# A list scheduler's price for entering the row strips: one figure for all, or one for the maxima and one for the exponentials

## The chip, the core and the metric

The kernel runs on one NeuronCore of a Trainium2 chip. The metric is the device time of one execution in microseconds (us). Three executions of the kernel before gave 1381.47, 1381.62 and 1383.63 us, median 1381.62.

## What is computed

The reference is one transformer layer on `x` of 2 x 2048 x 256 in float32: layer norm, causal attention with 16 heads of 16 (projections with biases, rotary positions), a residual sum, layer norm again, and a gated feed-forward of width 704 whose operands are rounded in blocks of 16 to a four-bit grid (E2M1), with another residual sum.

```python
x = x + attention(layernorm(x), Wq, bq, Wk, bk, Wv, bv, Wo, bo)
n = layernorm(x)
h = silu(fp4_linear(n, w_gate)) * fp4_linear(n, w_up)
x = x + fp4_linear(h, w_down)
# attention: softmax(mask(rope(q) @ rope(k).T / 4)) @ v, head by head
# fp4_linear(x, w) = fp4(x) @ fp4(w).T
```

## The kernel before, in words

The two sequences are cut into chunks of 512 rows, four for each, and the 16 heads into four groups of four. A slot is one group of one chunk; there are 32 of them. In each slot the scores are computed twice.

The first time they serve for the row maxima only (`max_steps`, called **the maxima** here). One task of this kind is two matmuls (line 1094, tile `sc`), one on the upper and one on the lower 64 rows of the TensorE array, each into a PSUM bank of its own. Two DVE reductions (line 1118) read the banks. At the diagonal four small masking matmuls (line 1062) belong to the task. When all maxima of a slot are found, DVE splits them into two bfloat16 parts, PE turns them (line 1175, tile `ptm`) and ACT copies them to `mT`.

The second time they are computed transposed, for the softmax (`value_steps`, called **the exponentials**). One task is two bfloat16 matmuls that subtract the maxima (line 1227) and two float32 score matmuls on top of them (line 1235), all on 64 rows, tile `sx`; ACT takes the exponential of both banks (line 1250). Four more matmuls (line 1283, tile `av`, **the values**) then multiply with `v` on all 128 rows and 32 columns each.

Everything else on PE (projections, turnings, the feed-forward's `pg` and `pd`) uses the whole array. A matmul thus runs in one of three tilings, named in the code `"strip"` (64 rows x 128 columns: maxima and exponentials), `"value"` and `"whole"`. All PSUM results but `av` rotate through seven banks; a task of maxima or exponentials takes two of them, other tasks one.

Nothing of this is issued as the loops run. Each step is given to `Plan.add` with its engine, a reckoned cost, what it reads and writes, its due time, and for PE the tiling. `Plan.ordered` is a list scheduler: it keeps a clock for each engine and a list of the tasks that are ready, and picks the next one. For the picked engine it takes the tasks that could begin within `PATIENCE` of the earliest, and of these the one with the smallest rank, the due time; on PE, `CHANGE` is added to a task whose tiling is not that of the task before. When a PE task does change the tiling, `ENTER[t.tiling]` is added to the reckoned start. The instructions of each engine are then issued in the order found and are tied to it. The engines run at their own pace; only the order is kept. Due times come from the place of the slot, so maxima of the next slot, exponentials of this one, projections and feed-forward are woven into each other.

In the first 170 us of the reckoned time, `kept_busy` (line 488) puts matmuls without use into PE time that the plan finds idle, one for each 0.2 us.

The figures that the change touches, as they stand before it:

```python
CHANGE = 0.1
PATIENCE = 0.03
ENTER = dict(strip=0.11, value=0.08, whole=0.08)
```

Of the kernel before, what the change touches and what calls it, by code (L numbers as in the profile page):

```python
# [65 lines left out]


AHEAD = 3
CHANGE = 0.1
FEED_M = 0.0  # L70
FEED_V = 0.0
PATIENCE = 0.03
TURN = 0.3
ISSUE = 0.46

# [29 lines left out]
PE, DVE, ACT, POOL, SP = "PE", "DVE", "ACT", "POOL", "SP"  # L105
# [6 lines left out]
    SP: {PE: 0.05, DVE: 0.05, ACT: 0.05, POOL: 0.05, SP: 0.05},  # L112
}

ENTER = dict(strip=0.11, value=0.08, whole=0.08)


class Thing:
# [13 lines left out]


class Task:
    __slots__ = "engine cost run due tiling late left ready end after new kinds start idle".split()


class Plan:
# [7 lines left out]

    def add(
        self, engine, cost, run, reads=(), writes=(), due=0.0, books=(), tiling="whole", feeds=0.0,
        late=0.0,
    ):  # L150
        t = Task()
        t.engine, t.cost, t.run, t.due = engine, cost, run, due - feeds

        t.tiling, t.late = tiling, late or 1.0 * (engine == SP)
        t.left, t.ready, t.end, t.after, t.new = 0, 0.0, None, [], []
        before = set()
        for thing in reads:
            assert thing.writers, (engine, due)
            before.update(thing.writers)
        for thing in writes:  # L160
            before.update(thing.writers)
            before.update(thing.readers)
        for thing in reads:
            thing.readers.append(t)
            thing.whole().users.append(t)
        for thing in writes:
            thing.writers, thing.readers = [t], []
            thing.whole().users.append(t)

        for thing in (*writes, *books):  # L170
            whole = thing.whole()
            if whole.kind and not whole.there:
                whole.there = True
                whole.users.append(t)
                whole.number = self.made[whole.kind] = self.made.get(whole.kind, -1) + 1
                t.new.append(whole)
        t.kinds = {}
        for thing in t.new:
            t.kinds.setdefault(thing.kind, []).append(thing)
        before.discard(t)  # L180
        for b in before:
            b.after.append(t)
        t.left = len(before)
        self.tasks.append(t)
        return t

    def ordered(self):

        waiting = {e: [] for e in HOP}
        for n, t in enumerate(self.tasks):  # L190
            if not t.left:
                waiting[t.engine].append((t.due, n, t))
        number = {t: n for n, t in enumerate(self.tasks)}
        free = dict.fromkeys(HOP, 0.0)
        rooms = {kind: [] for kind in ROOM}
        turn = dict.fromkeys(ROOM, 0)
        tiling = "whole"
        dues = sorted(((t.due, n) for n, t in enumerate(self.tasks)), reverse=True)
        done = set()
        out = []  # L200

        def vacancy(kind, n, to):

            held = rooms[kind]
            n -= ROOM[kind] - len(held)
            if n <= 0:
                return 0.0, []
            some = []
            for thing in held:
                if all(u.end is not None for u in thing.users):  # L210
                    at = max(
                        u.end + (u.late if u.engine != SP else 0.0) + HOP[u.engine][to]
                        for u in thing.users
                    )
                    some.append((at, thing.number, thing))
            if len(some) < n:
                return None
            some = sorted(some)[:n]
            return some[-1][0], [thing for *_, thing in some]

        while len(out) < len(self.tasks):
            while dues and dues[-1][1] in done:
                dues.pop()
            horizon = dues[-1][0] + (AHEAD if dues[-1][0] < self.near_end else 50.0)
            choice = None
            for e, queue in waiting.items():
                queue.sort(key=lambda x: x[:2])
                able = []
                vacant = {}
                for due, n, t in queue:  # L230
                    if due > horizon or len(able) > 30:
                        break
                    at = max(t.ready, free[e])
                    for kind, some in t.kinds.items():
                        if kind not in ANY_TURN and some[0].number != turn[kind]:
                            break
                        key = kind, len(some)
                        if key not in vacant:
                            vacant[key] = vacancy(*key, e)
                        if vacant[key] is None:  # L240
                            break
                        at = max(at, vacant[key][0])
                    else:
                        able.append((at, due, n, t))
                if not able:
                    continue
                first = min(at for at, *_ in able)
                if choice and first > choice[0] + 1e-9:
                    continue

                def rank(x):
                    at, due, n, t = x
                    return due + (CHANGE if e == PE and t.tiling != tiling else 0.0)

                pick = min((x for x in able if x[0] <= first + PATIENCE), key=rank)
                if choice is None or pick[0] < choice[0]:
                    choice = pick
            at, due, n, t = choice
            e = t.engine
            waiting[e].remove((due, n, t))  # L260
            for kind, some in t.kinds.items():
                for thing in vacancy(kind, len(some), e)[1]:
                    rooms[kind].remove(thing)
                rooms[kind] += some
                turn[kind] += len(some)
            if e == PE:
                if t.tiling != tiling:
                    at += ENTER[t.tiling]
                tiling = t.tiling
                t.start, t.idle = at, at - free[e]  # L270
            if e == SP:
                free[e] = at + ISSUE * t.late
                t.end = free[e] + t.cost
            else:
                t.end = free[e] = at + t.cost
            done.add(n)
            out.append(t)
            for a in t.after:
                a.left -= 1
                late = t.late if a.engine != e and e != SP else 0.0  # L280
                a.ready = max(a.ready, t.end + late + HOP[e][a.engine])
                if not a.left:
                    waiting[a.engine].append((a.due, number[a], a))
        self.span = max(t.end for t in out)
        return out
# [29 lines left out]
def layer_kernel(  # L315
# [88 lines left out]
    def lay_pick(due):  # L404
        def run():
            for strip in range(2):
                rows = slice(strip * STRIP, (strip + 1) * STRIP)
                nc.vector.tensor_copy(pick[rows], ident[rows, rows])

        add(DVE, 0.5, run, [fixed], [pick_], due)  # L410
# [660 lines left out]
    maxima, max_ = {}, {}  # L1071
# [3 lines left out]
    def max_steps(b, c, g):  # L1075
# [7 lines left out]
        def one(i, kc, d, due):  # L1083
# [22 lines left out]
            def reduced(h):  # L1106
# [21 lines left out]
                "strip",  # L1128
                FEED_M,
                0.07,  # L1130
            )
            for h in range(2):
                own = Thing(of=parts if c else mx)
# [60 lines left out]
        for i in range(TPC):  # L1194
            for kc in range(c + 1):
                for d in range(2):
                    steps.append(lambda due, i=i, kc=kc, d=d: one(i, kc, d, due))
# [529 lines left out]
    for n in range(slots + 1):  # L1727
        cost = 0.4 * (order[n // NG][1] + 1) if n < slots else 0
# [28 lines left out]
    for m in range(1, NBLK * len(order)):  # L1757
        k, blk = divmod(m, NBLK)
        at, use = place[2 * m - 2], place[2 * m]
# [21 lines left out]
    ready = [divided[NG * k + NG - 1] + 0.01 for k in range(len(order))]  # L1781
    ready[0] = max(ready[0], WEIGHTS + 0.2)
    end = place[slots + 1]
    at = 0
    for k in range(len(order) - 1):
# [3 lines left out]
        at = lo + (until - lo) / (last_k - k)  # L1789
        if NG * k + 10 < slots:  # L1790
            at = min(at, lo + (place[NG * k + 10] - lo) / 0.85)
        if k == len(order) - 2:
            at = end + LATE
# [6 lines left out]
    at = [0, 0, 1.5, 5.5, 8, 11, 12, 14.5, 17.3, 20, 26.7, 27.2, 28.2]  # L1800
# [167 lines left out]
```

## Time and profile before

| | |
|---|---|
| runs, us | 1381.47, 1381.62, 1383.63 (median 1381.62) |
| span of the profiled execution, us | 1378.9 |
| its own device time | not given apart from the runs; the median stands 2.7 us above the span |
| mean granted TensorE clock | 0.979 |
| PE busy | 1317.6 us, 96% |
| DVE busy | 1115.1 us, 81% |
| ACT busy | 749.9 us, 54% |
| GpSimd busy | 538.4 us, 39% |

PE is TensorE's matmuls, PEld its weight loads, which overlap the matmuls. Busy time of PE includes matmuls that overlap one another, so it does not show whether PE works at its best rate. The distances between the starts of successive matmuls show that better. In a timeline row, x2 or x4 says how many matmuls of one kind were merged, and the first number is the start of the first one.

### The profile page before, as it was taken

Reading aid. Unit: us, or ns where it says so; the run is one execution under the profiler, and the core shown is the slowest. Engines: PE = TensorE matmul, PEld = TensorE weight load, DVE = VectorE, ACT = ScalarE, POOL = GpSimd, SP = SyncE. Lnnn points to the kernel's source line nnn. Section 1 sums busy time; section 2 is a strip of 40 time slices with the busy share of each in tenths; the row PEclk is TensorE's granted clock in tenths of the full one; section 3 lists DMA queues with packets and bytes.
Section 4 is the critical chain, followed back from the end, with each engine's and each line's share of the span. In section 5 each row is a group of like instructions: output and inputs, shape, how many; then the busy total and the mean of one; then the engine's idle time right before and its main releaser. Section 6 shows DMA issues by size and latency. Waiting matters only on the chain.

```text
span 1378.9 us, 27730 instructions
## 1 busy us (share of the span) xinstructions
PE 1317.6 (96%) x10408; PEld 656.7 (48%) x10408; DVE 1115.1 (81%) x2415; ACT 749.9 (54%) x1670; POOL 538.4 (39%) x685
## 2 busy tenths in 40 slices
PE   7988999999999999999998999999999999999977
PEld 4544444444544444444454555444454444444445
DVE  7788989988889998875479888996878988894296
ACT  2542655556555566557643455554655566667711
POOL 4754634434423334314345644432442332320360
PEclk8998999999999999999999999999999999999988
DMA  2653432411221401221343414240130130000000
GB/s 88 133 134 100 103 94 58 104 33 55 62 41 44 107 20 41 64 45 51 89 113 94 108 44 97 66 95 22 47 86 17 43 81 13 9 9 9 9 1 19
DMA packets 61887, 84.39 MB, mean 61 GB/s; under 512 B 14772, under 2 KB 30520, under 8 KB 61752
## 3 DMA queue, kind: packets, MB, share of 16 engines
q1 hardware_dynamic: 61744, 82.61, 24.2%
q8 instruction: 82, 1.34, 0.4%
q14 instruction: 53, 0.43, 0.1%
q10 hardware_dynamic: 8, 0.00, 0.0%
HBM read 55.09 MB, written 27.49 MB: 60 GB/s over the span
## 4 chain that ended last, share of the span: by engine, by line
PE 65%; DVE 19%; POOL 5%; issue 5%; DMA 3%; ACT 2%; SPq 0%; POOLq 0%; DVEq 0%; ACTq 0%
PE av L1283 15%; PE sc L1094 9%; PE pg L1575 9%; PE sx L1227 8%; DVE parts L1118 7%; PE sx L1235 7%; PE pd L1669 6%; PE pj L837 3%; PE pth L1434 2%; PE po L1519 1%; PE pv L1019 1%; DVE scale L582 1%; DVE step L609 1%; DVE mx L1118 1%; PE sc L1062 1%
## 5 line engine op out<-in xcount | busy, mean ns | idle before, releaser
L1250 ACT ACTIVATE ex<-sx 128x512 f32<-128x512 f32 (+3 forms) x1280 | 592.8, 538 | 345.9 <-PE sx L1235 202.1
L1118 DVE TENSOR_REDUCE parts<-sc 128x1 f32<-128x512 f32 (+3 forms) x1152 | 637.9, 611 | 65.2 <-PE sc L1094 46.6
L1235 PE MATMUL sx<-qT,kT 64*128 64x512 f32 (+3 forms) x1280 | 335.6, 521 | 0.0
L1283 PE MATMUL av<-ex,v 128*32 128x512 f32 (+3 forms) x2560 | 301.3, 543 | 0.0
L1094 PE MATMUL sc<-kT,qT 64*128 64x512 f32 (+3 forms) x1280 | 280.3, 425 | 8.9 <-DMA kT<-parts 2.5
L1227 PE MATMUL sx<-mT,less 64*128 64x512 bf16 (+3 forms) x1280 | 246.5, 355 | 5.4 <-DVE parts L1118 1.6
L1094 PEld LDWEIGHTS sc<-kT,qT 64*128 64x128 f32 x1280 | 132.8, 188 | 168.1 <-DVE parts L1118 51.2
L1227 PEld LDWEIGHTS <-less 64*128 64x128 bf16 x1280 | 66.5, 94 | 213.3 <-issue 205.5
L590 POOL TENSOR_SCALAR inv<-inv 128x16 f32<-128x16 f32 (+2 forms) x82 | 17.7, 216 | 373.0 <-DVE inv L586 341.2
L1235 PEld LDWEIGHTS sx<-qT,kT 64*128 64x128 f32 x1280 | 131.3, 196 | 9.0 <-issue 6.8
L1669 PE MATMUL pd<-wdT,hrT 128*128 128x256 f32 (+1 forms) x384 | 103.9, 411 | 1.5 <-ACT hrT L1438 1.0
L1283 PEld LDWEIGHTS av<-ex,v 128*32 128x32 f32 x2560 | 52.6, 108 | 70.8 <-issue 60.4
L1669 PEld LDWEIGHTS pd<-wdT,hrT 128*128 128x128 f32 (+1 forms) x384 | 70.4, 197 | 29.1 <-issue 16.0
L889 POOL TENSOR_TENSOR t<-t,cs 128x512 f32<-128x512 f32 x31 | 39.9, 1286 | 110.2 <-DVE t L883 104.8
L1575 PE MATMUL pg<-wgT,xT 128*128 128x352 f32 x224 | 76.9, 476 | 0.9 <-ACT xT L1438 0.8
L837 PE MATMUL pj<-xnT,wqkT 128*128 128x512 f32 x128 | 73.8, 672 | 3.5 <-DVE v L1028 1.7
L1118 DVE TENSOR_REDUCE mx<-sc 128x1 f32<-128x128 f32 (+3 forms) x128 | 54.3, 477 | 25.8 <-PE sc L1062 25.8
L1575 PE MATMUL pg<-wuT,xT 128*128 128x352 f32 x224 | 74.4, 471 | 0.1
L1062 PE MATMUL sc<-pick,mask_q 64*128 64x64 bf16 x1024 | 67.3, 198 | 0.0
L615 POOL TENSOR_TENSOR h<-h,step 128x704 f32<-128x704 f32 x28 | 47.2, 1686 | 48.8 <-DVE step L612 41.0
L1601 ACT ACTIVATE h<-pg 128x352 f32<-128x352 f32 x64 | 29.9, 467 | 64.6 <-PE pg L1575 56.5
L547 POOL TENSOR_SCALAR ve<-mv 128x1 f32<-128x1 f32 x64 | 12.6, 197 | 130.4 <-DVE mv L543 127.1
(163 smaller groups left out, 1614.8 us busy)
## 6 DMA issues: line engine op xcount, KB each, us to landing
qT<-parts SPq DMA_DIRECT2D x120, 128.0 KB
kT<-parts SPq DMA_DIRECT2D x120, 128.0 KB
parts<-high SPq DMA_DIRECT2D x30, 256.0 KB
parts<-t SPq DMA_DIRECT2D x30, 256.0 KB
sums<-avs SPq DMA_DIRECT2D x28, 256.0 KB
cs<-in_rope_dram SPq DMA_DIRECT2D x8, 512.0 KB
xin<-in_L_attn_x_dram SPq DMA_DIRECT2D x28, 128.0 KB
y<-sums SPq DMA_DIRECT2D x28, 128.0 KB
```

The source lines that it names most:

```text
L615: queue.tensor_tensor(src(), src(), st["step"], ALU.add)
L837: nc.tensor.matmul(got["pj"], lhsT=wqkT[:, k, i, cols], rhs=xnTs[b, c][:, k, :], start=(k == 0), stop=(k == KE - 1),)
L889: (nc.gpsimd if early and i == 0 else queue).tensor_tensor(swapped, swapped, angles[b, c][:, 1, :], ALU.mult)
L1062: nc.tensor.matmul(sc[h][:, col + at : col + at + STRIP], lhsT=strips(mask, h, half), rhs=strips(pick, h), start=False, stop=(half == 1),)
L1094: nc.tensor.matmul(sc[h][:, :cols], lhsT=strips(qT, h, d, slice(i * P, (i + 1) * P)), rhs=strips(kT, h, duo, slice(0, cols)), start=True, ...
L1118: nc.vector.tensor_reduce(dst, got[0][h][:, :cols], AX.X, ALU.max)
L1227: nc.tensor.matmul(sc[h][:, off:], lhsT=strips(less[d], h), rhs=strips(mT, h, slice(off, CH)), start=True, stop=False,)
L1235: nc.tensor.matmul(sc[h][:, off:], lhsT=strips(kT, h, duo, slice(jj, jj + P)), rhs=strips(qT, h, d, slice(off, CH)), start=False, stop=(j ...
L1250: nc.scalar.activation(st[j, d][:, h, off:], got[0][h][:, off:], AF.Exp, scale=HD**-0.5)
L1283: nc.tensor.matmul(st["av"][SLOT * s : SLOT * (s + 1), off:], lhsT=v[:, at : at + SLOT], rhs=st[j, d][:, h, off:], start=(j == 0), stop=(j ...
L1575: nc.tensor.matmul(got[half], lhsT=split("xrT")[:, k, :], rhs=wT[:, k, half * IH : (half + 1) * IH], start=(k == 0), stop=(k == KE - 1),)
L1669: nc.tensor.matmul(st["pd"], lhsT=st["hrT"][:n, k, :], rhs=wdT[:n, k, :], start=(k == 0), stop=(k == KI - 1),)
```

## The change

The price of entering a tiling becomes a field of the task. A task of maxima now carries the figure `maxima`, 0.19; exponentials and the few other strip tasks carry `strip`, now 0.09 instead of 0.11. The ranking adds this price of the task itself where it added 0.1 to any change of tiling. `PATIENCE`, which holds for all engines, becomes 0.06. No instruction that computes is added or taken away; the order may change on all engines, and with it the useless matmuls of `kept_busy`.

```diff
-CHANGE = 0.1
 FEED_M = 0.0
 FEED_V = 0.0
-PATIENCE = 0.03
+PATIENCE = 0.06
...
-ENTER = dict(strip=0.11, value=0.08, whole=0.08)
+ENTER = dict(strip=0.09, maxima=0.19, value=0.08, whole=0.08)
...
     def add(
         self, engine, cost, run, reads=(), writes=(), due=0.0, books=(), tiling="whole", feeds=0.0,
-        late=0.0,
+        late=0.0, enter=None,
     ):
         t = Task()
+        t.enter = ENTER[enter or tiling]
...
-                    return due + (CHANGE if e == PE and t.tiling != tiling else 0.0)
+                    return due + (t.enter if e == PE and t.tiling != tiling else 0.0)
...
                 if t.tiling != tiling:
-                    at += ENTER[t.tiling]
+                    at += t.enter
...
                 "strip",
                 FEED_M,
                 0.07,
+                "maxima",
             )
```

More of the change, by code (lines that the diff above doesn't have):

```diff
@@ L134 @@
 class Task:
-    __slots__ = "engine cost run due tiling late left ready end after new kinds start idle".split()
+    __slots__ = "engine cost run due tiling late left ready end after new kinds start idle enter".split()
 class Plan:
```

## Prediction

> **What bounds the kernel.** I read the page first: the busy shares, then the chain of work that ended last, then the costliest groups.
>
> ```profile
> PE 1317.6 (96%) x10408; PEld 656.7 (48%) x10408; DVE 1115.1 (81%) x2415; ACT 749.9 (54%) x1670; POOL 538.4 (39%) x685
> ...
> PE 65%; DVE 19%; POOL 5%; issue 5%; DMA 3%; ACT 2%; SPq 0%; POOLq 0%; DVEq 0%; ACTq 0%
> ...
> L1250 ACT ACTIVATE ex<-sx 128x512 f32<-128x512 f32 (+3 forms) x1280 | 592.8, 538 | 345.9 <-PE sx L1235 202.1
> L1118 DVE TENSOR_REDUCE parts<-sc 128x1 f32<-128x512 f32 (+3 forms) x1152 | 637.9, 611 | 65.2 <-PE sc L1094 46.6
> ```
>
> PE carries most of the chain, DVE a fifth. One reduction takes 611 ns, one exponential 538, each twice per task. The busy time by stretches of 69 us shows where DVE is as full as PE:
>
> ```profile
> 207.00:276.00 69.00, 67.23 (x534) 33.48 (x532) 66.02 (x146) 35.38 (x80) 32.12 (x39) 1.00 0.36 81
> ...
> 414.00:483.00 69.00, 66.70 (x500) 31.88 (x496) 65.33 (x131) 38.41 (x81) 26.67 (x34) 1.00 0.31 76
> ...
> 1242.00:1311.00 69.00, 68.54 (x577) 30.77 (x574) 23.57 (x49) 51.19 (x116) 12.20 (x16) 1.00 0.03 9
> ```
>
> Columns are length, PE, PEld, DVE, ACT and POOL busy, clock, DMA share and rate. DVE leaves 3.0 and 3.7 us of 69 free in the first two, 45 in the last. So a gain on PE counts nearly everywhere, but in some stretches DVE stands close behind.
>
> The timeline of PE then shows what entering the strips costs:
>
> ```profile
> 488.12 0.39 PE L1094 MATMUL sc<-kT,qT 64*128 64x512 f32 x2
> 488.35 0.39 PE L1227 MATMUL sx<-mT,less 64*128 64x512 bf16 x2
> ...
> 488.91 1.13 PE L1519 MATMUL po<-woT,y 128*128 128x256 f32 x4
> 489.97 0.50 PE L1094 MATMUL sc<-kT,qT 64*128 64x512 f32 x2
> 490.32 0.39 PE L1227 MATMUL sx<-mT,less 64*128 64x512 bf16 x2
> 490.35 0.58 PE L1235 MATMUL sx<-qT,kT 64*128 64x512 f32 x2
> 490.77 0.40 PE L1094 MATMUL sc<-kT,qT 64*128 64x512 f32 x2
> 491.10 1.07 PE L1283 MATMUL av<-ex,v 128*32 128x512 f32 x8
> 492.10 0.39 PE L1227 MATMUL sx<-mT,less 64*128 64x512 bf16 x2
> 492.13 0.58 PE L1235 MATMUL sx<-qT,kT 64*128 64x512 f32 x2
> 492.55 0.40 PE L1094 MATMUL sc<-kT,qT 64*128 64x512 f32 x2
> ```
>
> From the first matmul of a task to that of the next, maxima inside strips take 0.23 (488.12 to 488.35); maxima behind a whole-array product take 0.35 (489.97 to 490.32). Exponentials take 0.45 in both cases (490.32 to 490.77 in strips, 492.10 to 492.55 behind the values). Medians over all such undivided tasks of 512 columns in the trace, taken the same way: maxima followed by exponentials 0.237 in strips (48 behind exponentials), 0.340 behind values (34) or whole (43); exponentials followed by maxima 0.458 in strips (43 behind maxima), 0.458 behind values (60) and whole (39). The change of tiling itself shows in the distance before: a last value matmul stands 0.433 from a next value task, 0.525 from exponentials, 0.522 from maxima. Leaving is alike: exponentials followed by values take 0.549 for 0.458. So each change costs 0.091, and maxima that enter cost 0.103 on top.
>
> **What the new order does.** The two programs' orders of PE, counted (useless matmuls as whole): strips are entered 528 times before, 256 by maxima and 272 by exponentials; after, 516 times, 120 and 396. Values are entered 310 and 318 times, whole 304 and 296. All changes: 1142 and 1130. The matmuls are the same, but for 140 useless ones instead of 139, so I take the clock as kept. Where work lies on the large scale hardly moves: after each further 128 value matmuls the counts of maxima differ by at most 8 of 1280, of feed-forward products by 3 or fewer, and what follows the last value is the same count.
>
> **Removed.** 136 fewer entries by maxima x 0.103 = 14.0 us. 12 fewer changes x 0.091 = 1.1 us. Sum -15.1 us, all on PE. The 124 entries that exponentials take over cost nothing beyond the change, counted already: they begin with two bfloat16 loads of 94 ns mean, while the maxima begin with float32 loads of 188 (rows of the weight loads). The Trainium skill's "TensorEngine Tiling (Array Packing)", section Key Properties, says that changing the tiling mode drains TensorE, and makes no difference by what enters. By that rule alone only the 12 changes would count, and the sum so far would be -1.1 us.
>
> **Added: waits for banks.** Exponentials first means maxima later and in clumps. Runs of a single task of maxima fall from 423 to 263, runs of two rise from 68 to 142, of three from 23 to 24, longer ones from 2 to 4. I took each task's excess over the quickest quarter of its like (same shape, same neighbours) in the trace: 113 us in all, of which 45 at seams among maxima, exponentials and values. Around a run of one the excess is 0.105 us, of two 0.226, of three 0.658. Priced so, the runs come to 76 us before and 78 after: +2. The other end: I counted, in both orders, how often one of the seven banks is wanted again after less unstalled PE work than its readers need (611 or 538 ns each, plus 0.35 for the hand-over by the kernel's own table). That is 246 times before and 302 after, 23% more, mostly at the exponentials. 23% of 45 us is +10. The waits of the weight loads say that such waits exist:
>
> ```profile
> PEld sc L1094 <- DVE parts L1118: 51.2, 83, 1.5
> PEld sc L1094 <- ACT ex L1250: 35.6, 65, 1.1
> ```
>
> They are time without a load, much of it hidden behind running matmuls, so not a price. I take +6, midway, since runs ignore what stands between them and the count ignores that one wait relieves the next. "TensorEngine Tiling (Array Packing)", section Gotcha 1: PSUM Pressure, speaks against the change in the same direction: row tiling puts more pressure on the banks. It gives no price.
>
> **Added: the end of a slot.** Behind the last maxima stand the split and the turning (line 1175), for which the first exponentials wait. PE has under 3 us of other work in between in 5 of 32 slots before, in 7 after. PE stood 5.3 us idle at line 1175 in all, about 1.06 for each short slot: 0 to +2, taken +1, as other slots gain room.
>
> **PATIENCE.** It lets the list reckon up to 0.03 us more idle time before a pick, on DVE, ACT, GpSimd and SP too. The engines themselves only follow the order, and no row prices that. Below: 0, where queued values and products cover it. Above: about 174 changed picks (124 entries and 50 more maxima inside strips) x 0.03 = +5. Taken 0, the nearer end, since a wait drawn only in the plan is none on the chip. Below nothing it could avoid a further change, but those are counted already. SP's queue swaps a few neighbours among `parts`, `xin` and weight loads, far ahead of their use; 0, unless a `qT` or `kT` comes late, as one 2.5 us wait of PE for `kT` did before.
>
> **Sum.** -15.1 + 6 + 1 + 0 = -8.1; ends -15.1 + 2 + 0 + 0 = -13.1 and -15.1 + 10 + 2 + 5 = +1.9. The span of 1378.9 becomes 1370.8, and with the same 2.7 around it the median becomes 1373.5; own range 1368.5 to 1383.5.
>
> **Rivals.** (1) Nothing is given back: exponentials that come earlier feed ACT, which is 46% idle, and the stalls stay. All 15.1 us arrive: 1366.5. For it: DVE has room in most stretches; against: 23% more short banks. (2) The gain dies off the path: only the chain's 65% PE and 5% issue carry it, -10.6, and the banks cost +10: -0.6, so 1381. (3) Slower: a pair of maxima holds four of seven banks, and the exponentials between are left three, so their next task waits for two exponentials of ACT, 2 x 0.538, against 0.458 of its own work: 0.62 us where nothing covers it. The orders have 74 more such pairs, at most +46. Half uncovered is +23, and -15.1 + 23 + 1 gives +9: 1390.5. It decides from 27 uncovered pairs on (17 us), since a measurement here can tell about 0.2%, 2.8 us, from no change. For it: ACT's 202 us of waiting for `sx` show that it lives from PE's pace. Against: values and products are queued between most of them, and the runs of two cost only 0.226 before. (4) That the change does nothing is excluded: 256 entries became 120.
>
> **Chances.** Forecast 0.46 (of it 0.42 faster by over 0.2%, 0.04 within), rival 1 0.22, rival 2 0.11, rival 3 0.21. Faster 0.42 + 0.22 = 0.64, within 0.04 + 0.11 = 0.15, slower 0.21. The range 1364 to 1388 takes in the ends of the forecast, rivals 1 and 2 and the milder part of rival 3; some 0.05 lies below and 0.13 above.
>
> **What would show it.** Right: in the new timeline maxima still take 0.237 and 0.340, entries by maxima are 120, and PE's excess grows by 4 to 12 us. Rival 1: excess unchanged at 113. Rival 3: excess above 130, the weight loads of lines 1094 and 1227 (now 1228) waiting longer for ACT's exponentials and DVE's reductions. Wrong altogether: if maxima inside strips come out at 0.34 as well, so that the price was never the entry's, or if one stretch alone, a late `kT` or a lower clock, holds the difference.

## The result, and the profile after

The changed kernel is slower: median 1395.36 us (1390.07 to 1398.74, 5 runs) beside 1382.93 of before, ratio 1.0073 with a 95% interval of 1.0047 to 1.0099. A second measurement beside another set of runs of before gave 1391.82 and 1.0067 (1.0037 to 1.0097). The prediction said 1373.5 and faster.

The page of the kernel after, the rows that answer to those of before:

```profile
PE 1327.0 (95%) x10409; PEld 670.1 (48%) x10409; DVE 1113.8 (80%) x2415; ACT 752.7 (54%) x1670; POOL 539.2 (39%) x685
...
PE 62%; DVE 21%; DMA 2%; issue 1%; ACT 1%; POOL 1%; SPq 0%; POOLq 0%; ACTq 0%; DVEq 0%
...
L1251 ACT ACTIVATE ex<-sx 128x512 f32<-128x512 f32 (+3 forms) x1280 | 595.4, 537 | 353.3 <-PE sx L1236 197.4
L1118 DVE TENSOR_REDUCE parts<-sc 128x1 f32<-128x512 f32 (+3 forms) x1152 | 635.8, 613 | 67.2 <-PE sc L1094 45.0
```

DVE and ACT do the same work in the same time. In the chain PE has a smaller share (62% after 65) and DVE a larger one (21% after 19). The clock by stretches, columns as in the prediction, two rows of after and then the second one of before:

```profile
69.00:138.00 69.00, 60.61 (x511) 35.16 (x510) 52.88 (x138) 21.32 (x52) 34.09 (x51) 0.85 0.46 116
...
1104.00:1173.00 69.00, 65.76 (x445) 31.62 (x444) 55.18 (x107) 35.60 (x77) 23.32 (x24) 0.88 0.21 45
```

```profile
1104.00:1173.00 69.00, 68.50 (x547) 32.77 (x545) 59.76 (x121) 42.32 (x93) 19.28 (x22) 1.00 0.19 47
```

The second stretch had full clock before. The mean granted clock of the profiled execution fell from 0.979 to 0.969.

The timeline of PE confirms the price of the entries:

```profile
488.98 1.06 PE L1284 MATMUL av<-ex,v 128*32 128x512 f32 x8
489.98 0.39 PE L1228 MATMUL sx<-mT,less 64*128 64x512 bf16 x2
490.02 0.58 PE L1236 MATMUL sx<-qT,kT 64*128 64x512 f32 x2
490.43 0.40 PE L1094 MATMUL sc<-kT,qT 64*128 64x512 f32 x2
490.67 0.39 PE L1228 MATMUL sx<-mT,less 64*128 64x512 bf16 x2
```

Exponentials now enter the strips and take 0.45 (489.98 to 490.43); the maxima behind them take 0.24. The medians are 0.458 and 0.238, and 0.338 to 0.340 for the few maxima that still enter: what they were.

**The account.** For each PE task of every trace I took the quickest quarter of its like (same shape, same kind of neighbours, at full clock) as its own time. What it took beyond that is a wait, except in stretches where the profile shows half the clock: there up to half of the task's time is put down to the clock. The quarters are those of all traces of this study together, with ordinary reductions and exponentials or with halved reductions; the prediction's 113 us of excess were waits and clock together. The four parts leave 12 to 14 us of each span undivided, 3 of them ahead of the first matmul. Each row is one execution; the half clock differs from one to the next. In us:

| profiled execution | span | own | waits | half clock | useless matmuls |
|---|---|---|---|---|---|
| before | 1378.9 | 1222.6 | 94.7 | 23.6 | 25.1 |
| after | 1391.0 | 1208.3 | 110.5 | 33.9 | 24.4 |
| after, again | 1390.3 | 1205.5 | 117.0 | 30.1 | 23.8 |
| ranking alone | 1407.3 | 1210.0 | 122.2 | 35.7 | 26.9 |
| last maxima ranked low | 1383.9 | 1208.0 | 116.3 | 21.6 | 24.6 |
| maxima due earlier | 1396.9 | 1206.9 | 131.3 | 22.4 | 23.6 |
| before, halved reductions | 1349.5 | 1220.5 | 72.0 | 22.0 | 21.3 |
| after, halved reductions | 1339.3 | 1205.1 | 88.9 | 9.5 | 23.8 |

PE's own work falls by 14.3 us, as forecast. Waits rise by 15.8 and the half clock costs 10.3 more; in the second trace of after it is 17.1, 22.3 and 6.5. Of the first trace's waits, 7.3 stand ahead of the turnings of the maxima (6.6 to 13.9), 6.3 at seams among maxima, exponentials and values (42.6 to 48.9), 4.3 where such tasks follow a side step, that is a projection, a turning or a product of the feed-forward (7.0 to 11.3).

**One place holds most of it.** I compared the times at which the 32 slots' values are copied out (counted from 0). Up to slot 26 the lag of after behind before wanders and stands at +3.3 us (+2.0 in the second trace). At slot 27 it jumps by 11.4 in both, to +14.7 and +13.4, and after the last slot 4 are regained. PE there, in the kernel after:

```profile
1105.28 0.97 PE L1094 MATMUL sc<-kT,qT 64*128 64x512 f32 x6
1106.18 0.64 PE L1284 MATMUL av<-ex,v 128*32 128x256 f32 x8
1108.49 0.38 PE L1176 MATMUL ptm<-ident_b,mslots 128*128 128x128 bf16 x4 [1.67 <-DVE t L857]
1109.71 3.18 PE L1094 MATMUL sc<-kT,qT 64*128 64x512 f32 x6 [0.84 <-DVE parts L1118]
1112.82 1.54 PE L1435 MATMUL pth<-ident,h 128*128 128x128 f32 x6
```

The turning of slot 28's maxima waits 1.67 us for DVE, the next maxima 0.84; before, neither waited there. Then the clock is halved from 1110.6 to 1127.7, 17 us, as the profile's clock records say: six turnings of `h` take 1.54 us here, 0.88 at 497.67 before. DVE ahead of it:

```profile
1102.80 0.52 DVE L609 TENSOR_SCALAR step<-h 128x704 int32<-128x704 int32 x1
1103.36 0.53 DVE L612 TENSOR_SCALAR step<-step 128x704 f32<-128x704 f32 x1
1103.80 0.21 DVE L1144 TENSOR_REDUCE mx<-parts 128x16 f32<-128x64 f32 x1
1104.04 1.71 DVE L1157 TENSOR_SCALAR mslots<-mx 128x16 int32<-128x16 int32 x1
1105.78 0.19 DVE L1160 TENSOR_TENSOR left<-mx,mslots 128x16 f32<-128x16 f32 x1
1106.00 1.55 DVE L1157 TENSOR_SCALAR mslots<-left 128x16 int32<-128x16 int32 x1
1107.59 0.19 DVE L1160 TENSOR_TENSOR mslots<-left,mslots 128x16 f32<-128x16 f32 x1
1107.69 0.74 DVE L857 SCALAR_TENSOR_TENSOR t<-pj,bqk,cs 128x512 f32<-128x512 f32 x1
```

and GpSimd at the same time:

```profile
1104.03 1.68 POOL L615 TENSOR_TENSOR h<-h,step 128x704 f32<-128x704 f32 x1 [1.68 <-DVE mx L1144]
1105.79 1.73 POOL L618 TENSOR_TENSOR h<-h,step 128x704 f32<-128x704 f32 x1
```

Two instructions of 16 elements take 1.71 and 1.55 us, and each ends as a GpSimd addition or subtraction of 704 elements ends. The split is done at 1107.78. The turning starts 0.71 us later still, when `t` ends, which reads a projection (`pj`) out of its PSUM bank. Before, the split stood ahead of the feed-forward's `step`, so GpSimd's two steps began only behind it:

```profile
1097.47 0.40 DVE L1156 TENSOR_SCALAR mslots<-mx 128x16 int32<-128x16 int32 x1
1097.90 0.18 DVE L1159 TENSOR_TENSOR left<-mx,mslots 128x16 f32<-128x16 f32 x1
1098.12 0.18 DVE L1156 TENSOR_SCALAR mslots<-left 128x16 int32<-128x16 int32 x1
...
1098.44 0.52 DVE L609 TENSOR_SCALAR step<-h 128x704 int32<-128x704 int32 x1
```

The new order puts `step` first on DVE, and the split pays 2.7 us for it (1.71 + 1.55 against 0.40 + 0.18). Over the whole trace of after, 43 of the 64 such instructions took under 0.25 us; the other 21 all overlapped a GpSimd instruction, and 20 of them ended within 0.05 us of its end. The Trainium skill's "SBUF — State Buffer", section Who interferes with whom, has this rule: a VectorE instruction in a two-port mode and a GpSimd instruction exclude each other, whichever came first holding the shared ports to its end. The rows agree, 1.71 beside 1.68, but no row tells the mode of the split's instruction. The two halves of the delay, the later place in DVE's queue and the longer instructions, were not parted by a run: I tried no split that keeps off those ports.

### The profile page after: what moved, and what is told of

It is laid out like the page before. It is cut to its first block, busy times and chain, and to the rows that moved or that the text cites. A ratio compares the mean times of both kernels' runs of the same rounds, so it can differ in the third digit from the quotient of the medians.

```text
span 1391.0 us, 27722 instructions
## 1 busy us (share of the span) xinstructions
PE 1327.0 (95%) x10409; PEld 670.1 (48%) x10409; DVE 1113.8 (80%) x2415; ACT 752.7 (54%) x1670; POOL 539.2 (39%) x685
## 4 chain that ended last, share of the span: by engine, by line
PE 62%; DVE 21%; DMA 2%; issue 1%; ACT 1%; POOL 1%; SPq 0%; POOLq 0%; ACTq 0%; DVEq 0%
PE av L1284 14%; PE pg L1576 10%; DVE parts L1118 9%; PE sx L1228 8%; PE sc L1094 8%; PE sx L1236 7%; PE pd L1670 5%; PE pj L837 2%; PE pth L1435 2%; PE pv L1019 1%; PE po L1520 1%; DVE scale L582 1%; DVE mslots L1157 1%; PE sc L1062 1%; DMA kT<-parts 1%
## 5 line engine op out<-in xcount | busy, mean ns | idle before, releaser
L1236 PE MATMUL sx<-qT,kT 64*128 64x512 f32 (+3 forms) x1280 | 344.2, 526 | 0.0
L1094 PE MATMUL sc<-kT,qT 64*128 64x512 f32 (+3 forms) x1280 | 269.7, 416 | 6.9 <-DVE parts L1118 3.0
L1228 PE MATMUL sx<-mT,less 64*128 64x512 bf16 (+3 forms) x1280 | 251.9, 358 | 6.7 <-ACT ex L1251 2.4
L1094 PEld LDWEIGHTS sc<-kT,qT 64*128 64x128 f32 x1280 | 140.3, 192 | 96.8 <-DVE parts L1118 31.3
L1576 PE MATMUL pg<-wgT,xT 128*128 128x352 f32 x224 | 80.5, 496 | 1.5 <-ACT ex L1251 1.0
L837 PE MATMUL pj<-xnT,wqkT 128*128 128x512 f32 x128 | 70.2, 651 | 2.3 <-DVE v L1028 1.8
L1062 PE MATMUL sc<-pick,mask_q 64*128 64x64 bf16 x1024 | 70.6, 200 | 0.0
L1062 PE MATMUL sx<-pick,mask_k 64*128 64x64 bf16 x1024 | 63.7, 198 | 0.0
```

The lines of the kernel that those rows point to most:

```text
L837: nc.tensor.matmul(got["pj"], lhsT=wqkT[:, k, i, cols], rhs=xnTs[b, c][:, k, :], start=(k == 0), stop=(k == KE - 1),)
L1062: nc.tensor.matmul(sc[h][:, col + at : col + at + STRIP], lhsT=strips(mask, h, half), rhs=strips(pick, h), start=False, stop=(half == 1),)
L1094: nc.tensor.matmul(sc[h][:, :cols], lhsT=strips(qT, h, d, slice(i * P, (i + 1) * P)), rhs=strips(kT, h, duo, slice(0, cols)), start=True, ...
L1228: nc.tensor.matmul(sc[h][:, off:], lhsT=strips(less[d], h), rhs=strips(mT, h, slice(off, CH)), start=True, stop=False,)
L1236: nc.tensor.matmul(sc[h][:, off:], lhsT=strips(kT, h, duo, slice(jj, jj + P)), rhs=strips(qT, h, d, slice(off, CH)), start=False, stop=(j ...
L1576: nc.tensor.matmul(got[half], lhsT=split("xrT")[:, k, :], rhs=wT[:, k, half * IH : (half + 1) * IH], start=(k == 0), stop=(k == KE - 1),)
```

## The experiments

The expectations set two theories against each other. By that of the slot ends, the new ranking finishes a slot's last maxima later, DVE splits them late, PE idles at the turning and the clock falls behind it. By that of clumps, maxima that come in pairs and triples wait for banks in the middle of the slots. Each kernel was measured beside runs of before of the same session.

**Which edit.** Each part alone. The first is one line:

```diff
-PATIENCE = 0.03
+PATIENCE = 0.06
```

> The kernel before with PATIENCE 0.06 alone; strips are entered 247 times by maxima (256 before), 1143 changes of tiling (1142). Theory of the slot ends (the new ranking finishes a slot's last maxima and their split later, PE idles at the turning of the maxima, and the clock is halved after the idle stretch): PATIENCE is not what costs, so 1380 to 1386, within 0.3% of before. Rival, PATIENCE itself costs: 1389 or more, most of the loss of the whole change.

Measured 1380.35 beside 1383.26, ratio 0.9978 (0.9958 to 0.9998). PATIENCE alone costs nothing; it gains a little.

```diff
-ENTER = dict(strip=0.11, value=0.08, whole=0.08)
+ENTER = dict(strip=0.09, maxima=0.19, value=0.08, whole=0.08)
...
-                    at += ENTER[t.tiling]
+                    at += t.enter          # rank: still CHANGE = 0.1, PATIENCE 0.03
```

> Only the reckoned start is changed (0.19 for maxima, 0.09 for exponentials); the ranking keeps 0.1 for any change and PATIENCE 0.03. Maxima enter 230 times, 1131 changes. Theory of the slot ends: the ranking is what moves the last maxima, so no loss here: entries give 26 x 0.103 + 11 x 0.091 = 3.7 us less, 1377 to 1384. Rival, any new order loses (waits for banks wherever the order is drawn anew): 1387 or more.

Measured 1379.86, ratio 0.9976 (0.9953 to 1.0000), as expected. A new order need not lose.

```diff
-                    return due + (CHANGE if e == PE and t.tiling != tiling else 0.0)
+                    return due + (t.enter if e == PE and t.tiling != tiling else 0.0)
...
                     at += dict(strip=0.11, value=0.08, whole=0.08)[t.tiling]   # as before
```

> Only the ranking is changed (0.19 for maxima, 0.09 for exponentials, 0.08 else); reckoning and PATIENCE as before. Maxima enter 133 times, 1157 changes: PE's own work 123 x 0.103 - 15 x 0.091 = 11.3 us less. Theory of the slot ends: the loss is here too, at the turning of the maxima and in the clock: 1388 to 1398. Rival, PATIENCE costs: 1370 to 1376. Rival, waits for banks spread over the whole course: 1388 to 1398 as well, but with no longer waits at line 1176.

Measured 1404.05, ratio 1.0158 (1.0137 to 1.0180), above the expected range. The ranking alone costs more than the whole change: 12.6 us of own work saved, 27.5 of waits and 12.1 of half clock added in the profiled execution. Slot 28's turning shows the same wait (1.66 us) and the same 17 us of half clock, and slot 27 adds 10.3 us to the lag. But 19.6 us of lag had gathered before it, so here that place holds only a part.

The two harmless parts together, with the old ranking:

```diff
-PATIENCE = 0.03
+PATIENCE = 0.06          # on top of the new ENTER in the reckoning, CHANGE = 0.1
```

> The new reckoning and the new PATIENCE together, with the old ranking (0.1 for any change); 236 entries by maxima, 1125 changes. If the ranking is the one costly part: both small gains add up, 1376 to 1382 beside a before of 1383. If the parts depend on each other's order: 1384 or more.

Measured 1391.08 beside 1382.80, ratio 1.0055 (1.0031 to 1.0078). That was a miss: the gains do not add up. Own work falls by 5.0, waits rise by 14.8. The mean clock of its runs, 0.979, is not below that of before, 0.978, so this loss is waits. Each change of a figure draws the whole order anew, and what that does to waits can outweigh the few microseconds of entries.

**Slot ends.** Maxima of the last quarter of each slot ranked like exponentials, all else as after:

```diff
                 "maxima",
+                0.09 if i == TPC - 1 else None,      # rank; the reckoned 0.19 stays
```

> The kernel after, but the maxima of a chunk's last 128 rows (the last quarter of each slot's) are ranked with 0.09 instead of 0.19, the reckoning as after; 150 entries by maxima, 1133 changes. Theory of the slot ends: the waits at the turning of the maxima fall by 3 us or more from after's 14, the half-clock time behind them too, 1382 to 1390. Theory of clumps (bank waits in the middle of the slots): little changes, 1391 to 1397.

Measured 1386.11, ratio 1.0033 (1.0010 to 1.0056): about half of what the change had lost comes back. PE in the profiled execution, at the place that cost 11.4 us:

```profile
1110.36 0.64 PE L1286 MATMUL av<-ex,v 128*32 128x256 f32 x8
1110.93 0.50 PE L1095 MATMUL sc<-kT,qT 64*128 64x512 f32 x2
1111.36 0.40 PE L1178 MATMUL ptm<-ident_b,mslots 128*128 128x128 bf16 x4
1111.59 1.08 PE L838 MATMUL pj<-xnT,wqkT 128*128 128x512 f32 x2
```

and DVE, where the split stands ahead of `step` again:

```profile
1107.45 0.40 DVE L1159 TENSOR_SCALAR mslots<-mx 128x16 int32<-128x16 int32 x1
...
1108.43 0.52 DVE L610 TENSOR_SCALAR step<-h 128x704 int32<-128x704 int32 x1
```

The turning does not wait, the clock stays full, and slot 27 adds 0.0 us to the lag. But the waits at turnings fall only from 13.9 to 12.5 in all, not by the 3 expected, since slots 0, 1, 4 and 19 still wait, and the lag stood at 8.2 us before slot 27 came.

The late split made by hand, in the order of before:

```diff
+                for _ in range({24: 8, 28: 8}.get(order.index((b, c)) * NG + g, 0)):
+                    nc.vector.tensor_reduce(...)    # the small reduction into mx, again
                 mx = st["mx"].rearrange("p i h d -> p i (h d)")
```

> The kernel before, in its order, with eight repeats of the small reduction ahead of the split in slots 24 and 28 (about 0.2 us each, 1.7 us of DVE in each slot). It makes by hand the late split that these slots have after. Theory of the slot ends with the clock: PE idles about 1 to 2 us longer at each turning, and the clock falls behind them in most runs: 4 to 14 us over before, the half-clock time up by 5 to 20 us. Without the clock: 2 to 4 us over before. If DVE catches up: 0 to 1.

Measured 1389.33, ratio 1.0050 (1.0028 to 1.0071), inside the range of the theory with the clock. PE in slot 28:

```profile
1109.68 1.10 PE L1094 MATMUL sc<-kT,qT 64*128 64x512 f32 x2 [0.99 <-DVE parts L1118]
...
1112.25 0.61 PE L1184 MATMUL ptm<-ident_b,mslots 128*128 128x128 bf16 x4
```

The sixteen repeats took 0.20 to 0.21 us each, 3.3 us of DVE in two places, and cost 6.5 us. The wait does not appear at the turning but ahead of it: the maxima at 1109.68 wait 0.99 us for a reduction. In slot 24 exponentials wait 1.21 us for DVE. The clock is halved for 10 us from 1112. So DVE being late costs about twice its length here, but at the banks, not at the turning.

**The clock.** Useless matmuls ahead of the turning in five slots, in the order of after and in that of before:

```diff
                 st["pt"] = bank
+                for _ in range({0: 5, 1: 12, 4: 20, 24: 14, 28: 14}.get(..., 0)):
+                    nc.tensor.matmul(bank..., lhsT=ident_b, rhs=mask_q..., start=True, stop=True)
```

> The kernel after, in its order, with 65 useless bfloat16 matmuls of 256 columns ahead of the turning of the maxima in the five slots where PE waited longer (5, 12, 20, 14 and 14 in the slots 0, 1, 4, 24 and 28). The waits themselves stay, but PE works through them. Theory of the slot ends with the clock: half-clock stretches behind these five go, 4 to 9 us less than after: 1386 to 1391. Theory of the slot ends without the clock, or waits for banks: 1394 to 1400, nothing gained or the matmuls' own time lost.

> The kernel before, in its order, with the same 65 useless matmuls in slots 0, 1, 4, 24 and 28, where its own waits are short (0.3 to 1.3 us). Theory of the slot ends with the clock: they cost their own time, 3 to 8 us more than before, and the clock gains little. If they help here as in the new order, 3 us less than before, the new order's waits there are not special.

In the order of after: 1392.05, ratio 1.0072 (1.0055 to 1.0089), between the two ranges and nothing gained. In that of before: 1383.77, ratio 1.0016 (0.9991 to 1.0040), 0.3 us more than before where 3 to 8 were expected. PE in the filled kernel, in the order of after:

```profile
1104.46 1.69 PE L1176 MATMUL ptm<-mask_q,ident_b 128*128 128x256 bf16 x14 [1.66 <-DVE t L857]
1105.99 0.39 PE L1184 MATMUL ptm<-ident_b,mslots 128*128 128x128 bf16 x4
```

So the edit did not do what it was meant to do. The useless matmuls read constants and write the turning's bank. In slot 28 PE waits for that bank 1.66 us, as long as without them, and then works 1.69 us on them. In slots 0, 4 and 24 it is alike (1.44, 2.86 and 1.84 us of idle time ahead of them); only in slot 1 do they run through the wait, of which 0.63 of 2.04 us is left.

Yet the clock stayed up. These windows of the filled kernel and of the kernel after end in clock, DMA share and rate:

```profile
1100.00:1120.00 20.00, 17.57 (x137) 10.09 (x136) 17.55 (x32) 8.04 (x23) 11.25 (x10) 1.00 0.30 84
```

```profile
1100.00:1120.00 20.00, 17.08 (x118) 9.30 (x116) 17.01 (x33) 6.37 (x19) 12.82 (x12) 0.77 0.06 14
```

The mean clock of its runs is 0.979, against 0.973 for the 15 runs of after. In the profiled execution, the quickest of its four (1384.93 us), the half clock costs 14.6 instead of 33.9, but the useless matmuls take 7.8 us more and the waits 6.7, and slot 27 still adds 6.9 us to the lag at full clock. What the clock gives, matmuls on top of the wait eat. What matmuls through the wait would do at slot 28, and with it how much of its 11.4 us is the clock's, stays open.

**Maxima first inside strips.** The new ranking, with all maxima due 0.1 earlier:

```diff
-FEED_M = 0.0
+FEED_M = 0.1
```

> The kernel after with all maxima due 0.1 earlier (FEED_M = 0.1): a change of tiling is ranked as after against staying, but maxima inside strips come before exponentials, so slots finish early; 118 entries by maxima, 1138 changes, PE's own work as low as after's. Theory of the slot ends: the turnings no longer wait, and most of the 14 us of PE's work arrive: 1368 to 1380. Theory of clumps: maxima still come in pairs and triples, the waits among maxima, exponentials and values are after's or more, 1385 to 1397.

Measured 1404.42, ratio 1.0165 (1.0133 to 1.0196), above both ranges. The slot ends are as before (7.4 us at turnings, half clock 22.4), and it is worse than after: seams among maxima, exponentials and values wait 62.6 us, 20 more than before. So there are two costs, and curing one by pulling all maxima forward raised the other.

**Whose waits.** Each reduction over half its columns, in three orders:

```diff
-                nc.vector.tensor_reduce(dst, got[0][h][:, :cols], AX.X, ALU.max)
+                nc.vector.tensor_reduce(dst, got[0][h][:, : cols // 2], AX.X, ALU.max)
```

> The kernel before, in its order, but each DVE reduction of the maxima reads only the first half of its columns, so it takes about 0.34 instead of 0.61 us and gives PE's banks back sooner. (The maxima are then those of half the scores.) If waits for DVE's banks are what bounds before beside PE's own work: 10 to 40 us less than before, 1343 to 1373. If only PE counts: 1378 to 1384.

> The kernel after, in its order, with the same halved reductions. Theory of banks and slot ends (DVE is late behind clumps of maxima, at the banks and at the split): with DVE twice as quick the waits go and PE's saved work shows, 8 to 16 us less than the halved before. Rival, the waits are on ACT's side (exponentials started in clumps), or the price of entering the strips was misread: equal to the halved before or slower.

> The kernel with maxima due 0.1 earlier, in its order, with the same halved reductions. It has the least work of PE itself and the most waits among maxima, exponentials and values. Theory of banks: 8 to 18 us less than the halved before, though with full reductions it was the slowest. Rival, waits on ACT's side: slower than the halved before.

Measured 1350.68 (1347.25 to 1351.84), 1344.10 (1341.13 to 1349.68) and 1366.27 (1363.07 to 1369.27), ratios to before 0.9751 (0.9709 to 0.9794), 0.9715 (0.9675 to 0.9756) and 0.9870 (0.9832 to 0.9908); one reduction of 256 columns took 381 ns on the mean. The 32 us that the halved reductions take from before lie in the range for waits on DVE's banks. With DVE quicker the order of after is 6.6 us faster than that of before, where it was 12.4 slower in the first measurement and 8.4 in the second. The sign turns, though the two sets of four runs touch and the gain is short of the expected 8. The clock turns too: half clock costs 9.5 us in the profiled execution of after (the quickest of its four) and 22.0 in that of before, the runs' mean clock is 0.986 against 0.9805, and slot 27 adds 4.6 us beside the halved before instead of 11.4. But the waits are still 16.9 us more than in the halved before, and the order with maxima due earlier stays the slowest. Its expectation under the theory of banks failed.

The other side, exponentials over half their columns, alone and together with the halved reductions. The values are then those of the first half, read twice:

```diff
-                    st[j, d][:, h, off:], got[0][h][:, off:], AF.Exp, scale=HD**-0.5
+                    st[j, d][:, h, off:mid], got[0][h][:, off:mid], AF.Exp, scale=HD**-0.5
```

> The kernel before, in its order, with each exponential taken over the first half of its columns only (about 0.33 instead of 0.54 us), and the value matmuls reading that half twice, so that their number and length stay. If ACT's banks are what PE waits for: 10 to 30 us less than before. If not: 0 to 5 less.

> The kernel after, in its order, with the same halved exponentials. If the new order's extra waits are for ACT's banks (exponentials that come right behind side steps and in clumps): 5 to 14 us less than the halved before. If they are DVE's: 6 to 14 us more than the halved before, as the full kernels.

> The kernel before, in its order, with both reductions and exponentials halved. Waits at banks small: 20 to 60 us less than before.

> The kernel after, in its order, with both halved. If banks and slot ends, held by DVE and ACT, are all that took the gain: 11 to 16 us less than the halved before, nearly the whole 14.5 us. If something else remains (GpSimd's feed-forward steps, transfers): less than 8 us.

Measured 1378.13 (1374.60 to 1384.56) and 1389.49 (1386.11 to 1392.13), with 352 ns for an exponential instead of 538. Before gains 6.0 us, between its two ranges; after is 11.4 us slower than before, as with full exponentials, so ACT does not hold the extra waits. Together 1344.72 (1338.42 to 1350.37) and 1339.44 (1337.94 to 1341.04): after 5.3 us faster, no more than with the reductions alone. These two sets of runs overlap, so the turn of the sign rests on both pairs with halved reductions pointing the same way. The loss thus hangs on DVE's time and not on ACT's; that DVE is late at the split, and not only at the banks, these runs do not tell apart. Less than 8 us of the 14 arrive even then, so by that expectation something else remains. In the traces with halved reductions PE stands idle for 3.7 us ahead of turnings of `h` for the feed-forward that follow maxima, and 0.0 in the order of before, but no run changes that alone. It stays open.

**A candidate.** The new reckoning alone, with useless matmuls at its four longest slot ends:

```diff
+                for _ in range({1: 8, 4: 20, 19: 18, 20: 6}.get(..., 0)):   # as above
```

> A candidate: the new reckoning alone (old ranking and PATIENCE), with useless matmuls ahead of the turning of the maxima in the slots 1, 4, 19 and 20 (8, 20, 18, 6), where that order's PE waited longest. If the clock falls behind those waits in most runs: 2 to 5 us less than the reckoning alone, 1375 to 1378. If not: 1379 to 1384.

Measured 1379.71 beside 1382.76, ratio 0.9960 (0.9936 to 0.9983). It beats both kernels, but by no more than the reckoning alone can be told to (0.9976); the expected further 2 to 5 us are not shown. In slots 1 and 19 the useless matmuls run through the wait (0.15 us is left in each), in slots 4 and 20 they stand behind it (2.85 and 0.99 us). The last run repeated the kernel after:

> The kernel after once more, beside before. By all measurements so far: 1391 to 1398, mean clock 0.967 to 0.977 against before's 0.975 to 0.981. If the earlier measurement was an outlier: under 1388.

Its 1391.82 and mean clock of 0.9735 lie where they were expected.

## Why the prediction was wrong

The own work was right: 15.1 us foretold, 14.3 and 17.1 in the two accounts, with 120 entries by maxima priced as before. What failed is what the prediction added to it: +7 us of waits (6 for banks, 1 for slot ends), and nothing for the clock. The two traces of after show 15.8 and 22.3 us of waits, and 10.3 and 6.5 of half clock. So 19 to 22 us more came back than was foretold, and that turned the sign.

**Waits for banks.** At the seams among maxima, exponentials and values +6 stands beside 6.3 in the first trace. But the prediction counted banks at those seams alone. Tasks that follow a side step wait 4.3 us more, and it had no term for them.

**The end of a slot** was a term, and mis-sized: +1 with an upper end of +2, measured +7.3. It counted PE's work between the last maxima and the turning, and priced each short slot by the mean idle time before. Slot 28 was not even short by that count (5.2 us before, 4.8 after). What was late was DVE: its split now stands behind the feed-forward's `step` and runs against GpSimd's steps. The prediction looked at the new order on PE and SP, and not at who stands ahead of the split on DVE. It also reckoned with the split alone ahead of a turning. In slots 0, 4, 24 and 28 of after the profile names as last another DVE instruction behind the split, one that reads a PSUM bank.

**The clock** was put at nothing: "The matmuls are the same, but for 140 useless ones instead of 139, so I take the clock as kept". The matmuls are the same, and the mean granted clock fell from 0.979 to 0.969: the half clock at slot 28 stands behind idle stretches that before did not have there. Over 84 runs of before taken in this study, time falls by 9.3 us for each 0.01 of mean clock (correlation -0.87). Mean clock 0.9772 there against 0.9727 in after's 15 runs makes, as an estimate, 4.2 us of a mean loss of 9.4; the profiled executions show 10.3 and 6.5. So the clock is the smaller part of the miss, and its exact size stays open. The page had said that it can happen: clocks of 0.88 to 0.90 in the first stretches of before, where PE stands idle.

Rival 3 was on the right side for the wrong reason, and that its 1390.5 comes near the measured time is luck. It laid the price on ACT's exponentials, and the halved exponentials excluded that. One of its signs came, an excess above 130 us (waits and half clock together make 144), the other did not: the weight loads of line 1094 waited 31.3 us for DVE's reductions after 51.2, and 15.1 for ACT's exponentials after 35.6. The PATIENCE term was right at 0 for itself, but not in company, as the pair of harmless parts shows. The prediction's sign of being wrong altogether, one stretch alone with a lower clock, came too: slot 27 with 11.4 of 12.1 us.

## What to carry to other kernels

When a hand-made scheduler's figures are corrected, the work that they price is saved and still not seen: check for each chain that ends a stage where its links now stand on every engine's queue, not on the bottleneck's alone. Price idle stretches of TensorE with the clock that follows them: two waits of 2.5 us together, with 17 us of half clock behind them, stood where 11 us were lost. Before filling a wait with useless matmuls, see what the wait is for; those that need the same bank wait as well. A better model of one cost need not give a better order, and two parts that each gained 0.2% lost 0.55% together.

## What the runs showed that was not expected

The time of an unchanged kernel followed its mean clock, from 1377.06 us at 0.985 to 1391.09 at 0.970. Half-clock stretches came in multiples of 3.4 us. In the two traces of after some came alike (17.1 us at slot 28, 6.8 us near 735 and near 769), others did not (17.1 us at 76.4 in one, 10.2 at 79.3 in the other).

The Trainium skill's "TensorE: Matmul & The Clock Gate", section What's actually happening, describes a window of that length that runs freely and two states, half and full. Its section Why this matters for your kernels asks for no idle gaps of over about 3 us. The measurement decides, and that is too mild here: idle stretches of 1.67 and 0.84 us, with one step of 0.38 us between them, were followed by 17 us of half clock in both traces of after.
